# A message-passing layer on one core: one pass over the nodes that writes both node tables

## The chip, the cores and the metric

The kernel runs on one core of a Trainium2 chip. The metric is device time in microseconds (us) of one execution. The kernel before took 5365.72 us, the median of three runs (5353.82, 5365.72 and 5367.68). A profiled execution of the same program, which the profile below describes, took 5379.39 us.

## The reference, cut to what matters

A graph has N = 12500 nodes with 96 features and E = 412500 directed edges, sorted by their destination. Each edge has four attributes.

```python
def _mlp(h, W, b, gamma, beta):
    h = relu(h @ W + b)
    mu, var = mean(h, axis=0), var(h, axis=0)          # over all rows
    return gamma * (h - mu) * rsqrt(var + EPS) + beta

node_feat = _mlp(x, W_node, ...)                        # 12500 x 96
edge_feat = _mlp(edge_attr, W_edge, ...)                # 412500 x 96
message = concatenate([x[row], x[col], edge_feat], 1)   # 412500 x 288
message = _mlp(message, W_msg, ...)
agg = segment_sum(message, col)
out = layernorm(x + agg + node_feat)
```

The product with `W_msg` splits into three blocks of 96 rows, one for the source node, one for the destination node, one for the edge's features. The first two need no edge: `x @ W_msg[0:96]` and `x @ W_msg[96:192]` are computed once for every node and read back by edge. These two products are the node tables, `p_tab` (by source) and `q_tab` (by destination).

## The kernel before, in words

All data is float32. TensorE handles a float32 product in two passes, so a product has two weight loads and two matmul records in the profile. The work has these parts, in the order in which TensorE does them.

1. **The source table** (`table`, lines 140 to 156, called at line 180). The nodes' features lie transposed in SBUF as `xp` (96 x 12544), loaded in seven parts of 14 blocks of 128 nodes. Each block is a stationary operand of 128 columns, and one 96 x 96 block of `w_msg` moves against it. Four blocks share one PSUM tile `pt` (four such tiles, one bank each). VectorE and ScalarE take turns to copy `pt` into the row tile `trow`, which holds 14 blocks (a chunk; three such buffers), and each chunk is written to `p_tab` with one DMA of 672 KB, from SP's queue and from ScalarE's in turn.
2. **A range check** (lines 205 to 219). The destinations `dst` are loaded, made relative to each block's base node (`rel`), reduced to one number on VectorE, transposed with one product on TensorE (`po`, line 216), and turned into a flag.
3. **The destination table** (`table` once more, line 333). It does the same with the second block of `w_msg`, into `q_tab`, with all seven writes from SP's queue. Some 128 rows of zeros are then written around its ends (lines 337 to 340).
4. **Positions** (`places`): four loads, four subtractions on VectorE and four writes to `rel_d`.
5. **The node features** (`nodes`): 25 products `pn` (line 248), a ReLU on ScalarE, statistics on VectorE, the normalised result added to `xp`, then 98 products `py` in groups of eight (line 262), copied as `y0s` and written to `y0_d` (line 269).
6. **The edge statistics** (`edge_norm`, lines 273 to 325): 606 products of 512 columns (`pr`, line 290). Two of them share a tile, on which ScalarE does a ReLU (line 294) and VectorE two `bn_stats` (line 296); such a pair is the unit of this part, 303 in all. Their input `ea` is loaded for eight blocks at a time (line 284), into two buffers.
7. **The messages** (lines 498 to 530): 202 steps, written out by hand for all engines. Each step takes four groups of 512 edges through `edges`, `linear` (z), `message` and `sums`.
8. **The end** (lines 701 to 734): the normalised sum is added to `y0_d`, normalised by row and written.

Beside all this runs GpSimd (POOL). It fetches rows of a table by the edges' source numbers with indirect DMAs, 128 rows each (line 162), called gathers below. The first 26 blocks of 16 gathers go through two `stage` buffers to a scratch area `spill` in DRAM, with one write of 768 KB for each block on SP's queue (line 173). The first three blocks fetch rows of `x` itself; the other 23 fetch from `p_tab` and so wait for all of its seven writes. After the 26 blocks come 100 gathers into a ring of 25 tiles for the first message steps. In the message loop POOL goes on gathering into the ring as its tiles come free.

The orders of SP and POOL are written out by hand in the program (`manual_schedule`); those of TensorE, VectorE and ScalarE before the message loop are made by a scheduler that keeps the program's order nearly everywhere. `next(store)` emits the next block, that is its 16 gathers on POOL and its write on SP, at that place of the two queues. SP works its queue strictly in order: a `spill` write stands behind the loads and writes ahead of it, and those behind it wait until its block has been gathered. A block's gathers need the stage buffer of the block two before, and so that block's write. Each queue issues a DMA only when an earlier one on the same of eight semaphores has landed. In `edge_norm` a block is emitted at 17 of the 26 yields.

Of the kernel before, what the change touches and what calls it, by code (L numbers as in the profile page):

```python
# [11 lines left out]
F32 = mybir.dt.float32  # L12
I32 = mybir.dt.int32
AF = mybir.ActivationFunctionType
# [3 lines left out]
PSUM = bass.MemoryType.PSUM  # L18
DRAM = bass.MemoryType.DRAM

N, C, E, ED = 12500, 96, 412500, 4
EPS = 1e-5
P = 128
# [3 lines left out]
GT, GE, BG = 4, 512, 4  # L27
# [12 lines left out]
NN = NB * P  # L40
NBK = 4
CH = 14
# [5 lines left out]
WN, WS, WM = 31, 16, 7  # L48
# [24 lines left out]
def gnn(ctx, tc, t):  # L73
    nc = tc.nc
    const = ctx.enter_context(tc.tile_pool(name="const", bufs=1))
    dram = ctx.enter_context(tc.tile_pool(name="dram", bufs=1, space=DRAM))
    p_tab = dram.tile([NN, C], F32, name="p_tab")
    q_tab = dram.tile([WT, C], F32, name="q_tab")
# [6 lines left out]
    w_msg = const.tile([C, 3, C], F32, name="w_msg")  # L85
# [4 lines left out]
    xp = xpool.enter_context(tc.tile_pool(name="x", bufs=1)).tile([C, NN], F32, name="xp")  # L90
# [46 lines left out]
        return s[:, 0:1], s[:, 1:2]  # L137


    def table(out, w, work, ps, queues, bufs):  # L140

        rows = out.rearrange("(b p) f -> p b f", p=P)
        for c in range(0, NB, CH):
            r = work.tile([P, CH, C], F32, name="trow", bufs=3)
            for j, i in enumerate(range(0, CH, NBK)):
                n = min(NBK, CH - i)
                pt = ps.tile([P, NBK, C], F32, name="pt", bufs=bufs)
                for g in range(n):
                    k = (c + i + g) * P
                    nc.tensor.matmul(pt[:, g, :], xp[:, k:k + P], w, start=True, stop=True)  # L150
                if j % 2:
                    nc.scalar.activation(r[:, i:i + n, :], pt[:, :n, :], AF.Copy)
                else:
                    nc.vector.tensor_copy(r[:, i:i + n, :], pt[:, :n, :])
            queues[c // CH % len(queues)].dma_start(rows[:, c:c + CH, :], r)
            yield

    def gather(g, pg):
# [17 lines left out]

    store = blocks()
    with tc.manual_schedule(engines={ET.SP, ET.Pool}):
        with tc.tile_pool(name="win_w", bufs=1) as work, tc.tile_pool(name="win_ps", bufs=2, space=PSUM) as ps:
            for i, _ in enumerate(table(p_tab, w_msg[:, 0, :], work, ps, (nc.sync, nc.scalar), 4)):  # L180
                if i in (2, 5):
                    next(store)

    zero = const.tile([64, C], F32, name="zero")
# [5 lines left out]
    for i in range(NS):  # L190
        k, n = Q * i, C - Q * i
# [7 lines left out]
    with tc.tile_pool(name="win", bufs=1) as win, tc.tile_pool(name="win_ps", bufs=2, space=PSUM) as ps:  # L199
# [11 lines left out]
        out = win.tile([P, 1], F32, name="out")  # L211
# [115 lines left out]
    def fast(ring):  # L327
# [1 line left out]
            return gather(g, ring.tile([P, GT, C], F32, name="pg"))  # L329

        with tc.manual_schedule(engines={ET.SP, ET.Pool}):
            with tc.tile_pool(name="tab_w", bufs=1) as work, tc.tile_pool(name="tab_ps", bufs=2, space=PSUM) as ps:
                for i, _ in enumerate(table(q_tab[WM:WM + NN, :], w_msg[:, 1, :], work, ps, (nc.sync,), 8)):
                    if i in (0, 2, 5):
                        next(store)
            next(store)
            nc.sync.dma_start(q_tab[:WM, :], zero[:WM])
            for r in range(WM + NN, WT, 64):
                n = min(64, WT - r)
                nc.sync.dma_start(q_tab[r:r + n, :], zero[:n])  # L340
            places()
            for i, _ in enumerate(nodes()):
                if i in (0, 4, 10):
                    next(store)
            xpool.close()
            n = 0
            for i, _ in enumerate(edge_norm()):
                if 73 * i >= 50 + 100 * n:
                    next(store, None)
                    n += 1  # L350
            for _ in store:
                pass
            got = {g: ahead_of(g) for g in range(SPILL, SPILL + RING)}
# [347 lines left out]
    with tc.tile_pool(name="fin", bufs=2) as work, tc.tile_pool(name="fin_ps", bufs=2, space=PSUM) as ps:  # L701
# [9 lines left out]
        out = t["out"]  # L711
# [57 lines left out]
```

## Time and profile before

| | |
|---|---|
| median of three runs | 5365.72 us |
| the profiled execution's own time | 5379.39 us |
| its span in the profile | 5377.6 us |
| PE busy (matmul records) | 3364.1 us, 63% |
| POOL busy | 3106.6 us, 58% |
| VectorE (DVE) busy | 1699.3 us, 32% |
| ScalarE (ACT) busy | 1077.6 us, 20% |
| DMA, mean | 50 GB/s |
| gathers from a table | 3175, some 0.95 us each |

The busy shares are means over stages that differ. The table of stretches that the prediction shows is read in this way: the stretch in us, its length, then busy time and number of instructions of PE, the weight loads, DVE, ACT and POOL, then the granted TensorE clock, the share of the DMA engines and GB/s. In a list by time, each line has the start, the length, engine, line and tile; the bracket at its end is the time that the engine stood idle before it, and what ended that. "issue" means that nothing in the profile explains the idle time, "remote" that the releasing event could not be assigned.

### The profile page before, as it was taken

Reading aid. Unit: us, or ns where it says so; the run is one execution under the profiler, and the core shown is the slowest. Engines: PE = TensorE matmul, PEld = TensorE weight load, DVE = VectorE, ACT = ScalarE, POOL = GpSimd, SP = SyncE. Lnnn points to the kernel's source line nnn. Section 1 sums busy time; section 2 is a strip of 40 time slices with the busy share of each in tenths; the row PEclk is TensorE's granted clock in tenths of the full one; section 3 lists DMA queues with packets and bytes.
Section 4 is the critical chain, followed back from the end, with each engine's and each line's share of the span. In section 5 each row is a group of like instructions: output and inputs, shape, how many; then the busy total and the mean of one; then the engine's idle time right before and its main releaser. Section 6 shows DMA issues by size and latency. Waiting matters only on the chain. (4 is left out here: it accounts for less than half of the span.)

```text
span 5377.6 us, 46715 instructions
## 1 busy us (share of the span) xinstructions
PE 3364.1 (63%) x16705; PEld 2570.3 (48%) x16705; DVE 1699.3 (32%) x2622; ACT 1077.6 (20%) x1015; POOL 3106.6 (58%) x3244
## 2 busy tenths in 40 slices
PE   5566662666656666665667666656666666666668
PEld 5333330354545545544445554544455545545447
DVE  1445551622222322222222322322232222223225
ACT  0224441411111111111111111111111111111112
POOL 5454456155566656666666666666666666666661
PEclk9755555566666766667676766666766666666667
DMA  5332332111111111111111111111111111111112
GB/s 165 112 97 61 71 68 48 29 33 37 39 44 38 43 42 44 43 38 42 42 43 45 42 38 43 44 42 45 37 43 42 41 45 36 43 43 42 44 37 84
DMA packets 188578, 270.80 MB, mean 50 GB/s; under 512 B 121095, under 2 KB 121480, under 8 KB 187330
## 3 DMA queue, kind: packets, MB, share of 16 engines
q0 software_dynamic: 103136, 158.62, 12.2%
q1 hardware_dynamic: 77120, 98.40, 6.6%
q10 hardware_dynamic: 8080, 10.71, 0.7%
q8 instruction: 133, 2.18, 0.2%
q14 instruction: 109, 0.89, 0.1%
HBM read 225.90 MB, written 41.60 MB: 50 GB/s over the span
## 5 line engine op out<-in xcount | busy, mean ns | idle before, releaser
L162 POOL DMA_INDIRECT pg<-p_tab,src x2807 | 2690.8, 959 | 1767.1 <-DVE hs L463 922.8
L448 PE MATMUL z<-rhs,left 128*128 128x96 f32 x6446 | 1222.7, 339 | 878.3 <-issue 672.8
L448 PEld LDWEIGHTS z<-rhs,left 128*128 128x128 f32 x6446 | 1093.2, 249 | 1183.6 <-issue 903.1
L480 PE MATMUL pa<-h 128*97 128x128 f32 x6446 | 1246.3, 331 | 556.2 <-issue 551.6
L480 PEld LDWEIGHTS pa<-h 128*97 128x97 f32 x6446 | 1015.4, 209 | 654.7 <-issue 653.3
L463 DVE TENSOR_TENSOR hs<-z,pg 128x384 f32<-128x384 f32 x702 | 385.2, 555 | 2599.2 <-remote 1537.6
L465 ACT ACTIVATE h<-hs 128x768 f32<-128x768 f32 x402 | 338.9, 843 | 2867.6 <-DVE hs L463 1846.0
L290 PE MATMUL pr<-ea,wide 10*128 10x512 f32 x1212 | 405.4, 1074 | 285.7 <-issue 177.6
L162 POOL DMA_INDIRECT stage<-p_tab,src x368 | 351.0, 954 | 369.6 <-DMA spill<-stage 240.0
L440 ACT ACTIVATE left<-pr 96x2048 f32<-96x2048 f32 x202 | 377.2, 1867 | 643.6 <-remote 439.7
L441 DVE TENSOR_SCALAR left<-pr 31x2048 f32<-31x2048 f32 x202 | 462.9, 2291 | 108.3 <-ACT left L440 75.5
L296 DVE BATCH_NORM_STATS2 estats<-r 128x6 f32<-128x512 f32 x606 | 365.8, 678 | 326.8 <-issue 191.1
L433 PE MATMUL pr<-ea,we 6*127 6x512 f32 x1404 | 411.1, 808 | 62.6 <-issue 47.5
L290 PEld LDWEIGHTS pr<-ea,wide 10*128 10x128 f32 x1212 | 209.6, 320 | 480.2 <-issue 291.8
L294 ACT ACTIVATE r<-pr 128x1024 f32<-128x1024 f32 x303 | 297.1, 1024 | 458.0 <-remote 290.0
L433 PEld LDWEIGHTS pr<-ea,we 6*127 6x127 f32 x1404 | 117.9, 223 | 206.6 <-issue 190.6
L457 DVE TENSOR_TENSOR h<-rel,iota 128x496 f32<-128x496 f32 x202 | 134.6, 666 | 0.0
L463 DVE TENSOR_TENSOR hs<-z,pb 128x384 f32<-128x384 f32 x104 | 56.6, 554 | 233.1 <-remote 85.2
L150 PE MATMUL pt<-w_msg,xp 96*128 96x96 f32 x392 | 88.7, 421 | 60.4 <-issue 37.1
L493 DVE TENSOR_TENSOR agg<-pa,agg 97x62 f32 x404 | 90.1, 223 | 85.4 <-remote 54.8
L150 PEld LDWEIGHTS pt<-w_msg,xp 96*128 96x128 f32 x392 | 85.5, 330 | 63.4 <-issue 48.6
L494 DVE TENSOR_TENSOR gram<-pa,gram 97x388 f32<-97x388 f32 x202 | 111.4, 551 | 0.1
(107 smaller groups left out, 634.7 us busy)
## 6 DMA issues: line engine op xcount, KB each, us to landing
pg<-p_tab,src POOLq DMA_INDIRECT x2807
spill<-stage SPq DMA_DIRECT2D x26, 768.0 KB
pb<-spill SPq DMA_DIRECT2D x26, 768.0 KB
ea<-in_ea SPq DMA_DIRECT2D x75, 160.0 KB
rhs<-q_tab SPq DMA_DIRECT2D x202, 46.5 KB
ea<-in_ea SPq DMA_DIRECT2D x352, 20.0 KB
stage<-p_tab,src POOLq DMA_INDIRECT x368
q_tab<-trow SPq DMA_DIRECT2D x7, 672.0 KB
```

What stands on the lines that cost most here:

```text
L150: nc.tensor.matmul(pt[:, g, :], xp[:, k:k + P], w, start=True, stop=True)
L162: nc.gpsimd.indirect_dma_start(out=pg[:, i, :], out_offset=None, in_=tab[:, :], in_offset=bass.IndirectOffsetOnAxis(ap=idx[:, k:k + 1], ax ...
L290: nc.tensor.matmul(pr[:, k % 2, :], wide[Q * i:Q * i + 2 * EK, :], ea[Q * i:Q * i + 2 * EK, b % J, :], start=True, stop=True)
L294: nc.scalar.activation(r, pr, AF.Relu)
L296: nc.vector.bn_stats(stats[:, (k - o) % NS, (k - o) // NS, :], r[:, 1 - o, :])
L433: nc.tensor.matmul(prs[s][:C + WN, i, :], we[Q * i:Q * i + EK + 1, :], block[s][Q * i:Q * i + EK + 1, :], start=True, stop=True)
L440: nc.scalar.activation(x[:C, :n, :], pr[:C, :n, :], AF.Relu)
L441: nc.vector.tensor_scalar(x[C:C + WN, :n, :], pr[C:C + WN, :n, :], 0.0, None, op0=OP.is_equal)
L448: nc.tensor.matmul(zs[k][:, i, :], left[s % 2][:KR, g % BG, i * P:(i + 1) * P], rhs[:KR, s % RB, g % BG, :], start=True, stop=True)
L463: nc.vector.tensor_add(hs[:, i % 2, :n, :], z[:, :n, :], pg[:, :n, :])
L465: nc.scalar.activation(h[:, i - 1:i + 1, :, :C], hs, AF.Relu)
L480: nc.tensor.matmul(pas[s][:, g % BG, :C + 1 + WN], h[:r, i, :C + 1], h[:r, i, :C + 1 + WN], start=i == 0, stop=i == n - 1)
```

## The change

Both tables are made in one pass. The two 96-column blocks of `w_msg` lie side by side and move together, 192 columns, against each stationary block of nodes. A PSUM tile is now two banks (still four blocks of nodes, four such tiles, so all eight banks), and each copy carries both tables' rows for its blocks. The row tile holds both tables and has two buffers instead of three. Each chunk is written with two DMAs of 672 KB, one for each table, one from SP's queue and one from ScalarE's, in turn. The places of the blocks' gathers and writes in the orders of SP and POOL move as well: before the edge statistics eight blocks are emitted instead of nine, so 18 instead of 17 come in them. The zero rows of `q_tab` and with them the load of `dst` follow the last table write.

```diff
-    def table(out, w, work, ps, queues, bufs):
-        rows = out.rearrange("(b p) f -> p b f", p=P)
+    def tables(work, ps):
+        outs = [t.rearrange("(b p) f -> p b f", p=P) for t in (p_tab, q_tab[WM:WM + NN, :])]
+        w = w_msg[:, 0:2, :].rearrange("k s f -> k (s f)")
         for c in range(0, NB, CH):
-            r = work.tile([P, CH, C], F32, name="trow", bufs=3)
+            r = work.tile([P, CH, 2, C], F32, name="trow", bufs=2)
             for j, i in enumerate(range(0, CH, NBK)):
                 n = min(NBK, CH - i)
-                pt = ps.tile([P, NBK, C], F32, name="pt", bufs=bufs)
+                pt = ps.tile([P, 2, GE], F32, name="pt")
                 for g in range(n):
                     k = (c + i + g) * P
-                    nc.tensor.matmul(pt[:, g, :], xp[:, k:k + P], w, start=True, stop=True)
+                    nc.tensor.matmul(pt[:, g // 2, g % 2 * 2 * C:(g % 2 + 1) * 2 * C], xp[:, k:k + P], w,
+                                     start=True, stop=True)
+                to = r[:, i:i + n, :, :].rearrange("p (k b) s f -> p k (b s f)", b=2)
                 if j % 2:
-                    nc.scalar.activation(r[:, i:i + n, :], pt[:, :n, :], AF.Copy)
+                    nc.scalar.activation(to, pt[:, :n // 2, :4 * C], AF.Copy)
                 else:
-                    nc.vector.tensor_copy(r[:, i:i + n, :], pt[:, :n, :])
-            queues[c // CH % len(queues)].dma_start(rows[:, c:c + CH, :], r)
+                    nc.vector.tensor_copy(to, pt[:, :n // 2, :4 * C])
+            for k in range(2):
+                (nc.scalar if (c // CH + k) % 2 else nc.sync).dma_start(outs[k][:, c:c + CH, :], r[:, :, k, :])
             yield
...
-        with tc.tile_pool(name="win_w", bufs=1) as work, tc.tile_pool(name="win_ps", bufs=2, space=PSUM) as ps:
-            for i, _ in enumerate(table(p_tab, w_msg[:, 0, :], work, ps, (nc.sync, nc.scalar), 4)):
-                if i in (2, 5):
+        with tc.tile_pool(name="win_w", bufs=1) as work, tc.tile_pool(name="win_ps", bufs=4, space=PSUM) as ps:
+            for i, _ in enumerate(tables(work, ps)):
+                if i in (2, 4):
                     next(store)
...
         with tc.manual_schedule(engines={ET.SP, ET.Pool}):
-            with tc.tile_pool(name="tab_w", bufs=1) as work, tc.tile_pool(name="tab_ps", bufs=2, space=PSUM) as ps:
-                for i, _ in enumerate(table(q_tab[WM:WM + NN, :], w_msg[:, 1, :], work, ps, (nc.sync,), 8)):
-                    if i in (0, 2, 5):
-                        next(store)
-            next(store)
             nc.sync.dma_start(q_tab[:WM, :], zero[:WM])
             for r in range(WM + NN, WT, 64):
                 n = min(64, WT - r)
                 nc.sync.dma_start(q_tab[r:r + n, :], zero[:n])
+            next(store)
             places()
+            next(store)
+            next(store)
             for i, _ in enumerate(nodes()):
-                if i in (0, 4, 10):
+                if i in (1, 5, 10):
                     next(store)
```

## The prediction

> **What bounds the kernel now.** I read the chain of waits first; it covers only the last 1%. So I cut the span into the program's parts and read busy times by stretch (columns: PE, PEld, DVE, ACT, POOL, then clock, DMA share, GB/s).
>
> ```profile
> 0.00:87.00 87.00, 43.68 (x196) 42.26 (x196) 8.33 (x20) 6.82 (x15) 46.67 (x56) 1.00 0.66 177
> 87.00:174.00 87.00, 45.35 (x197) 43.30 (x197) 19.46 (x28) 5.22 (x14) 47.71 (x48) 1.00 0.41 123
> 174.00:226.00 52.00, 30.71 (x50) 9.54 (x50) 20.59 (x33) 18.51 (x28) 30.85 (x32) 0.73 0.42 131
> 226.00:305.00 79.00, 43.71 (x196) 42.26 (x196) 36.32 (x26) 13.37 (x10) 30.27 (x32) 0.50 0.30 106
> 305.00:915.00 610.00, 338.89 (x994) 171.51 (x996) 297.07 (x496) 239.66 (x245) 336.77 (x356) 0.50 0.31 68
> 915.00:995.00 80.00, 66.51 (x220) 38.05 (x216) 64.23 (x109) 55.62 (x57) 0.00 (x0) 0.50 0.16 31
> 995.00:1047.00 52.00, 7.37 (x36) 5.24 (x36) 32.66 (x34) 4.02 (x4) 0.83 (x1) 0.50 0.03 9
> 1047.00:5300.00 4253.00, 2728.80 (x14486) 2160.80 (x14486) 1182.12 (x1802) 715.27 (x611) 2595.40 (x2707) 0.68 0.16 41
> ```
>
> The change touches the first 995 us only. The message loop (1047 to 5300) keeps its instructions in their order on every engine. The stretches are: source table, destination table, node features (two), edge statistics while POOL still gathers, the same after POOL's end (915), its closing sums, and the loop. The page's share "PE 63%" is thus a mean mostly over the loop; here PE was busy for half of the two table stretches.
>
> Next, PE by time, with the destination table.
>
> ```profile
> 107.47 29.75 PE L150 MATMUL pt<-w_msg,xp 96*128 96x96 f32 x138 [0.37 <-DVE most L218]
> ...
> 152.92 0.32 PE L150 MATMUL pt<-w_msg,xp 96*128 96x96 f32 x1 [2.48 <-issue]
> ...
> 165.54 8.41 PE L150 MATMUL pt<-w_msg,xp 96*128 96x96 f32 x38 [0.18 <-issue]
> 174.37 18.80 PE L248 MATMUL pn<-xp,w_node 96*96 96x512 f32 x36 [0.42 <-ACT trow L152]
> ```
>
> From 107.47 there are 138 passes in 29.75 us, 0.216 us each. Then one pass comes only every 2.8 us for "issue", and from 165.54 it is dense again. POOL's gathers at that time:
>
> ```profile
> 87.57 0.94 POOL L162 DMA_INDIRECT stage<-p_tab,src  x1 [18.26 <-DMA we<-step]
> ...
> 120.57 0.95 POOL L162 DMA_INDIRECT stage<-p_tab,src  x1 [11.00 <-DMA spill<-stage]
> ...
> 159.35 0.95 POOL L162 DMA_INDIRECT stage<-p_tab,src  x1 [0.30 <-issue]
> 175.58 0.95 POOL L162 DMA_INDIRECT stage<-p_tab,src  x1 [15.29 <-DMA spill<-stage]
> ```
>
> A gather starts every 1.25 us from 120.57 to 160.3. PE thins out 17 us after this train began and recovers 5 us after its end. The same holds in the source table, on DVE (train to 69.3):
>
> ```profile
> 38.80 1.02 DVE L154 COPY trow<-pt 128x384 f32<-128x384 f32 x2 [10.85 <-DMA p_tab<-trow]
> ...
> 56.81 0.56 DVE L154 COPY trow<-pt 128x384 f32<-128x384 f32 x1 [14.84 <-remote]
> 74.45 1.02 DVE L154 COPY trow<-pt 128x384 f32<-128x384 f32 x2 [17.08 <-remote]
> ```
>
> The copies at 56.81 and 74.45 waited 15 and 17 us; after the train ended all went on. Edge statistics, two stretches of 10 us:
>
> ```profile
> 480.00:490.00 10.00, 2.07 (x4) 0.51 (x4) 1.29 (x2) 1.02 (x1) 7.56 (x9) 0.50 0.16 39
> 600.00:610.00 10.00, 10.00 (x38) 5.85 (x37) 10.00 (x18) 8.63 (x10) 0.00 (x0) 0.50 0.10 14
> ```
>
> With POOL gathering, ten us hold 4 PE records, that is one pair; with POOL idle, 38. In the thin mode a pair takes 11.2 us, in the dense one 1.19 us (212 records, 53 pairs, in the 62.94 us from 931.96). I call this the thin mode: it sets in 12 to 17 us after a long train begins and ends 5 us after it. Its cause is not in the profile. It means that work beside POOL's trains is nearly stopped, and that the early part lasts about as long as the trains (468 gathers after `p_tab`, 585 us) plus the dense work outside them.
>
> **The change part by part.** I count against the profiled 5379.4 us (span 5377.6, 1.8 outside), which is 13.7 above the median of 5365.7; the saving is then taken off the median.
>
> *Products.* 392 passes of 96 columns become 196 of 192. A `pn` pass (512 moving columns, 96 stationary) took 18.80/36 = 0.522 us. Against 0.216 this is 0.307 us for 416 columns more, so 96 more cost 0.07 to 0.08, bounded by 0 and by 0.216 (nothing saved). I take 0.29 a pass, 0.58 a product, 8.1 us for a chunk of 14, where one table's chunk took 6.0. In sum 57 us instead of 85.
>
> *Copies.* 56 become 28 of double width. On DVE the `y0s` copy has just this shape and took 0.947 us, against 0.557: 14 x 0.947 = 13.3 instead of 15.6. On ACT 768 columns lie between 0.491 (384) and 1.024 (1024 columns); I take 0.80: 9.0 instead of 11.5. They lie beside the next products (8.1 us a chunk against 1.9 and 1.3). Without that cover they add some 2 us a chunk.
>
> *Writes and buffers.* The 14 writes stay, seven now on each queue. With two row buffers a chunk's first copy waits for both writes of the chunk two before. Before, with three, the first such wait was 10.85 us long (38.80), for a write issued at 33.74: 5 us to landing. That write stood behind small constant loads on SP; one more load now stands ahead of it (0.4 us). So chunk 2 is copied at about 40, although its products are done by 9.0 + 3 x 8.1 = 33. From there each chunk needs 8.1 us of PE; two chunks (16.2) cover copies, issue and landing (3 + 0.4 + 5), so writes add nothing unless landing takes 13 us. Four more chunks of products and their last copies end near 40 + 5 x 8.1 = 81, landed 86, against the first gather from `p_tab` at 87.57.
>
> The skill's page "Perfetto Trace Analysis", section Optimization Strategy, speaks against this part: repeated bubbles on the engine that should be full can mean too few buffers for the next tile. By it five chunks would each show a wait; at 15 us to landing it would be 1.1 us a chunk, 5 us in all, where the row of 5 us gives none.
>
> The page "TensorE: Matmul & The Clock Gate", Part 1, has the array at half clock until some 3.4 us of sustained work. Passes here stayed at 0.216 us for 29.75 us on end, while eight `z` passes of the same width took 0.87 us at 1116.22. By the page, warm passes would take some 4 us off each of five chunks, 20 us in all, an estimate; the sum keeps the measured rate.
>
> *The thin mode in this stage.* Before, 27 us passed between 47.3 and 74.45 with 16 of 196 passes done. The third raw block now has to wait for the first block's spill write, which moved behind chunk 2's write (issued at 37.76 before, now at 43 or later), so POOL's train breaks for some us near 50. Between no stretch (86) and the old one kept whole (113) I take half: `p_tab` complete at 99, +11.4 us.
>
> *The second table's stage goes.* From the first gather (87.57) to `pn` (174.37) were 86.8 us, of which 20 (load of `dst`, reductions, `po` until 107.47) stay, as PE still runs `po` ahead of `pn`. So 66.8 us go. The zero rows' three writes (1 us each) stand ahead of `dst` now, but it waits for the table writes to land anyway. `pn` starts at 99 + 20 = 119 instead of 174.4: -55.4.
>
> *Node features* took 131 us (174.37 to 305) beside 64 gathers. They now meet a train from 99 to 139 (blocks 3 and 4), whose spill writes stand behind the positions' writes on SP, and a second from some 146 to 186. Passes still owed at 2.8 us would add up to 25 us; against that, PE at 107.47, also 20 us into a train, ran dense. The first two `y0_d` writes wait for block 4's spill (near 141), while before they were ready 17 us after the statistics, here past 180: hidden. I take +10 (0 to 25). Edge statistics start at 260 instead of 305: -45.
>
> *Edge statistics* get one block more, 16 gathers, 20 us. A lone train costs the thin part, 20 - 13 + 5 = 12 us. The upper bound is a whole period: from 387.09 to 550.80 POOL's starts are five blocks apart, 33 us each. The lower bound is 0, as the trailing 80 us without POOL (915 to 995) could take it. I take +12. POOL's end moves by -45 and one period, 33, to 903, the statistics' to 995 - 45 + 12 = 962; so POOL isn't late for the loop, where it waited 131 us.
>
> Sum: +11.4 - 66.8 + 10 + 12 = -33 us. 5365.7 - 33 = 5333.
>
> **The rivals.**
>
> *More is won* (5298 to 5318): no thin stretch in the table stage (-13) and none new in the node features (-10). For it: the broken train. Against: POOL starts the same 48 raw gathers at the same time.
>
> *Nothing is won* (5350 to 5380): the 67 us held 40 us of gathers, which must go elsewhere and slow what stands there. Old thin stretch kept (+14), node features +25 instead of +10, gives -4: 5362. Here belongs also that a wide pass costs two narrow ones (0.43): four or five chunks x 4 us, -15.
>
> *Slower*: the node products fall into the thin mode. 50 passes at 2.8 us are 140 us instead of 50; with +90 in place of +10 the sum is +47: 5413. It decides from some 26 passes more than the 14 that were thin before (33 + 10 + 16 = 59 us, at 2.28 us extra a pass). For it: they now start 20 us into a 40 us train. Against: after block 6 (near 186) POOL must wait for a spill that stands behind the first two `y0_d` writes, so the mode is broken twice.
>
> **How the numbers follow.** Three runs of the kernel differ by 0.26%, so about 0.3% (16 us) can be told from no change. Chances: forecast (5318 to 5349) 0.48, more won 0.21, nothing won 0.19, slower 0.12. All low costs together give 5365.7 - 33 - 13 - 10 - 12 = 5298; run scatter puts the end at 5293. The upper end, 5375, takes in nothing won but for its highest edge cost (+21 on -4 would be 5383); with the slower case and what lies below 5293 some 0.2 are left out. Faster 0.69, same 0.19, slower 0.12.
>
> **What would show it.** Right: 196 table passes of about 0.29 us; the first gather from `p_tab` between 86 and 113; `pn` 20 us after it; the first `pr` product near 260; the last one near 962; loop of the same length, 33 us earlier. Wrong: `pn` records 2.8 us apart for more than 50 us; DVE copies waiting over 13 us for table writes at each chunk; POOL's last ring gather after the edge statistics; a loop that differs by over 15 us.

## The result and the profile after

The changed kernel took 5296.60 us, the median of four runs (5291.13 to 5302.76); the kernel before took 5361.52 us beside it. The ratio is 0.9884, with a 95% interval of 0.9868 to 0.9900, so 65 us were won. The forecast was 33 us. The profiled execution has a span of 5294.2 us.

The stretches of the changed kernel, in the columns of the table shown for the kernel before (stretch, length, PE, weight loads, DVE, ACT, POOL, clock, DMA share, GB/s), cut at the same events:

```profile
0.00:81.00 81.00, 41.76 (x196) 39.80 (x196) 13.92 (x20) 10.17 (x15) 46.56 (x57) 0.81 0.94 251
81.00:102.00 21.00, 0.40 (x2) 0.10 (x2) 11.55 (x14) 0.00 (x0) 16.43 (x16) 0.50 0.51 154
102.00:142.00 40.00, 28.34 (x50) 9.11 (x50) 17.21 (x26) 14.33 (x21) 30.55 (x32) 0.71 0.54 171
142.00:244.00 102.00, 43.71 (x196) 42.26 (x196) 41.28 (x40) 17.43 (x16) 55.49 (x60) 0.50 0.35 105
244.00:883.00 639.00, 369.49 (x1092) 184.84 (x1092) 324.99 (x538) 261.75 (x269) 342.21 (x363) 0.50 0.32 68
883.00:935.00 52.00, 37.06 (x120) 19.79 (x120) 35.71 (x60) 31.71 (x33) 0.00 (x0) 0.50 0.08 13
935.00:983.00 48.00, 4.00 (x18) 2.03 (x18) 31.10 (x32) 3.33 (x4) 0.00 (x0) 0.50 0.03 6
983.00:5240.00 4257.00, 2823.15 (x14640) 2204.56 (x14639) 1196.81 (x1836) 719.48 (x618) 2583.14 (x2707) 0.68 0.18 41
```

The first line now holds all passes for both tables: 196, as many as the source table alone had, and PE is busy for 41.76 us where it was for 43.68. The next one, 21 us, is all that is left between the first gather from `p_tab` and the node products; it was 86.8 us. TensorE by time, changed kernel:

```profile
9.55 10.28 PE L151 MATMUL pt<-w_msg,xp 96*128 96x192 f32 x44 [9.55 <-DMA xp<-in_xp]
...
39.94 16.95 PE L151 MATMUL pt<-w_msg,xp 96*128 96x192 f32 x84 [5.58 <-DVE trow L157]
58.60 6.50 PE L151 MATMUL pt<-w_msg,xp 96*128 96x192 f32 x28 [1.71 <-DVE trow L157]
...
101.98 20.17 PE L252 MATMUL pn<-xp,w_node 96*96 96x512 f32 x40 [0.37 <-DVE most L222]
```

The first 44 wide passes came in 10.28 us, 0.234 each, and the last four chunks (112 passes) in 25.2 us, with one wait of 1.71 us between. There is no thin stretch on TensorE. POOL's list by time, same execution:

```profile
53.37 0.94 POOL L166 DMA_INDIRECT stage<-in_x,src_raw  x1 [5.88 <-DMA spill<-stage]
...
80.96 0.94 POOL L166 DMA_INDIRECT stage<-p_tab,src  x1 [7.93 <-issue]
```

The third raw block had to wait 5.88 us (from 47.5) for the first block's spill write, which SP had issued at 41.99. So the raw train broke, and the first gather from `p_tab` started at 80.96 in place of 87.57. Of the thin mode one long wait was left, in ScalarE's last copy, with the last table write behind it (ScalarE by time):

```profile
73.81 0.49 ACT L155 ACTIVATE trow<-pt 128x384 f32<-128x384 f32 x1 [8.66 <-remote]
74.33 0.46 ACTq L159 DMA_DIRECT2D q_tab<-trow  x1
```

Where the time went, by stage. The last columns are from the experiments below: one profile of the kernel before (e9) and two of the changed kernel (e5, e10) on a second chip, where the kernel before takes 5392 to 5396 us. Each entry is a difference of two start times read from the lists by time.

| stage | forecast | recorded runs: before, after | change | second chip: before | after (e5, e10) | change |
|---|---|---|---|---|---|---|
| start to first gather from `p_tab` | +11.4 | 87.6, 81.0 | -6.6 | 89.2 | 85.3, 82.1 | -4.0, -7.1 |
| to first `pn` | -66.8 | 86.8, 21.0 | -65.8 | 87.7 | 21.2, 21.1 | -66.5, -66.6 |
| to first `pr` (node features) | +10 | 135.4, 142.3 | +6.9 | 125.4 | 174.9, 172.8 | +49.6, +47.4 |
| to the end of the last wide `pr` | +12 | 685.1, 690.5 | +5.4 | 695.9 | 682.2, 682.5 | -13.7, -13.4 |
| to first `z` | 0 | 48.4, 47.9 | -0.5 | 48.4 | 47.8, 47.8 | -0.6 |
| sum at first `z` | -33 | 1043.3, 982.7 | -60.6 | 1046.5 | 1011.3, 1006.3 | -35.2, -40.2 |
| loop, to `norm_msg` | 0 | 4279.6, 4256.9 | -22.7 | 4294.0 | 4286.7, 4300.9 | -7.3, +6.9 |

In the recorded runs 60.6 us are there when the message loop starts, against 65 us between the medians. The profiled execution of before was a long one (5379.4 against a median of 5361.5); if these 18 us lie in its loop, they are most of the loop's -22.7. Two profiles of one program differ by 14 us in that row (e5, e10).

### The profile page after: what moved, and what is told of

Same layout as the page of the kernel before. It is cut to its first block, busy times and chain, and to the rows that moved or that the text cites. A ratio compares the mean times of both kernels' runs of the same rounds, so it can differ in the third digit from the quotient of the medians.

```text
span 5294.2 us, 46278 instructions
## 1 busy us (share of the span) xinstructions
PE 3390.6 (64%) x16509; PEld 2544.8 (48%) x16509; DVE 1697.4 (32%) x2608; ACT 1071.9 (20%) x1001; POOL 3092.4 (58%) x3244
## 5 line engine op out<-in xcount | busy, mean ns | idle before, releaser
L482 PE MATMUL pa<-h 128*97 128x128 f32 x6446 | 1230.0, 331 | 473.0 <-issue 470.2
L435 PE MATMUL pr<-ea,we 6*127 6x512 f32 x1404 | 508.9, 883 | 92.6 <-issue 79.8
L435 PEld LDWEIGHTS pr<-ea,we 6*127 6x127 f32 x1404 | 144.5, 242 | 291.0 <-issue 278.8
L735 POOL TENSOR_TENSOR y<-y,sd 128x768 f32<-128x768 f32 (+1 forms) x13 | 18.0, 1394 | 107.7 <-DVE sd L734 105.7
L435 PE MATMUL pr<-eae,we 6*127 6x512 f32 x208 | 64.7, 820 | 10.8 <-issue 9.7
```

The costliest lines, as they stand in the source:

```text
L435: nc.tensor.matmul(prs[s][:C + WN, i, :], we[Q * i:Q * i + EK + 1, :], block[s][Q * i:Q * i + EK + 1, :], start=True, stop=True)
L482: nc.tensor.matmul(pas[s][:, g % BG, :C + 1 + WN], h[:r, i, :C + 1], h[:r, i, :C + 1 + WN], start=i == 0, stop=i == n - 1)
```

## The experiments

Two theories of the source table's stage are set against each other. TRAINS: what is done beside a train of gathers older than some 15 us is slowed to the thin mode, so it matters where POOL's trains are cut. FEWER PASSES (first named FEWER INSTRUCTIONS): the gain is TensorE's work that is no longer done. For the later stages the rival of TRAINS is LOAD: the number of gathers costs what it costs, wherever and however long they run.

The chips differed more than the kernels. The kernel before took 5392 to 5396 us on the second chip (e5 to e12) and 4164 to 4165 us on two others (e1 to e4; e13 to e18), where the thin mode was not found. The first expectations had not reckoned with that. The chip of the recorded runs has no number on record; that it is not the second one is read from the times alone, 5353.8 to 5367.7 us there against 5374.2 to 5410.8 on the second.

### e1, two products; e2, early spill; e3, late spill in the kernel before; e4, three row buffers (no thin mode)

```diff
# e1: for each node block, on the changed kernel
-nc.tensor.matmul(pt[:, g // 2, g % 2 * 2 * C:(g % 2 + 1) * 2 * C], xp[:, k:k + P], w, ...)
+for s in range(2):
+    o = (g % 2 * 2 + s) * C
+    nc.tensor.matmul(pt[:, g // 2, o:o + C], xp[:, k:k + P], w_msg[:, s, :], ...)
# e2: on the changed kernel           # e3: on the kernel before
-    if i in (2, 4):                  -    if i in (2, 5):
+    if i in (1, 3):                  +    if i in (4, 5):
# e4: on the changed kernel
-RING = 25                            -r = work.tile([P, CH, 2, C], F32, name="trow", bufs=2)
+RING = 21                            +r = work.tile([P, CH, 2, C], F32, name="trow", bufs=3)
```

> One pass over the nodes as in the changed kernel, the same copies and writes, but two products of 96 columns for each node block in place of one of 192. TRAINS (the table pass became quick because POOL's gathers were cut into trains of 18 to 20 us): the pass count matters only by its dense cost. 392 passes at 0.216 us are 85 us against 196 at 0.234 (46 us, 44 passes in 10.28 us in the changed kernel), so a chunk costs 12.1 us instead of 6.6. The first gather from the source table moves from 81.0 to about 105, as five chunks lie behind the first wait; the total is 20 to 28 us above the changed kernel, about 5320. FEWER INSTRUCTIONS (it became quick because half as many passes were left to be thinned out): passes 2.8 us apart appear in the table pass, the first gather comes at 115 or later, the total is 35 us or more above, 5332 or more.

> The changed kernel with the first two blocks emitted one and one chunk earlier, so that the first spill write stands ahead of the third chunk's write and POOL's raw gathers run on without a pause from 29 to about 70, as in the kernel before. TRAINS: thin mode returns from about 45 to 75, copies on VectorE and ScalarE wait 12 us or more there, the first gather from the source table moves from 81 to 91 to 100, and the total is 8 to 18 us above the changed kernel: 5305 to 5315. FEWER INSTRUCTIONS: no such waits, first gather at 78 to 84, total 5293 to 5300.

> The kernel before, both tables in two passes, with only the first block emitted two chunks later, so that its spill write stands behind the fifth chunk's write and POOL pauses after 32 raw gathers (about 48 to 58). TRAINS: the waits of 15 and 17 us on VectorE vanish, the first gather from the source table comes at 72 to 80 instead of 87.6, the total falls by 7 to 15 us against the kernel before. FEWER INSTRUCTIONS: thin mode stays, first gather at 85 or later, the total within 5 us of the kernel before.

> The changed kernel with three row buffers instead of two; to make room the ring has 21 tiles instead of 25, so the message loop is not to be compared, only the table pass. BUFFERS BIND: TensorE's idle time in the table pass (5.4, 5.6 and 1.7 us before the passes at 32.7, 39.9 and 58.6) goes, the table pass ends 8 to 12 us sooner (last pass at 53 to 57 instead of 65.1). BUFFERS DO NOT BIND, as the prediction said: the writes' queue sets the pace, the last pass comes at 61 to 66.

The kernel before took 4163.84 us. e1: 4182.10 (ratio 1.0047, 1.0031 to 1.0064). e2: 4157.38 (0.9985, 0.9976 to 0.9995). e3: 4164.98 (1.0003, 0.9993 to 1.0013). e4: 4160.82 in a single run. With no thin mode there is nothing for TRAINS to act on, so these runs leave it open. They show that the change is worth little there (6.5 us in e2) and that two narrow products lose it and more. With a third row buffer the last wide pass ended at 61.0, against 62.5 in e2 and 64.9 in e16 (the changed kernel as it is, on the other chip without the thin mode), and the first gather from `p_tab` came at 75.27, against 73.46 and 74.25. So the third buffer moves the passes by 1.5 to 4 us and nothing behind them; e4's whole time has a smaller ring in it and is not to be compared. In e1 the first gather from `p_tab` stood at 100.26 against 73.46 in e2, 26.8 us later; the end came 24.7 us later.

### e5 and e10, the changed kernel; e9, the kernel before (second chip)

No edit.

> The changed kernel once more, with nothing altered, to see what the change is worth on the chip that these runs are on. Two answers are prepared, told apart by the time of the kernel before in the same call. If the kernel before takes near 5360 us there (TensorE, VectorE and ScalarE issue one pass in some 2.8 us beside long trains of gathers, the thin mode): ratio 0.985 to 0.991, 48 to 80 us won, first gather from p_tab at 78 to 84 us, first pn pass at 98 to 106, first pr pass at 235 to 255. If the kernel before takes near 4164 us (no thin mode): the second table's stage was 43 us of dense passes there (80 to 123 us) on TensorE, while GpSimd's gathers set the end, so 2 to 12 us won, ratio 0.997 to 0.9995, first gather from p_tab at 72 to 80 us, first pn pass near 95, first pr pass near 197. The theory that the gain is TensorE work removed (196 passes by 0.21 us, 42 us) wants 35 to 45 us won on either chip.

> The kernel before, unaltered, for one profile on the chip of these runs, so that the change can be read stage by stage on a second chip. If its time is above 5300 us: first gather from p_tab at 80 to 92 us, first pn pass at 170 to 195, first pr pass at 300 to 335, first z pass at 1035 to 1065. Theory STAGES (the gain is the second table's stage and the first gather, and the node and edge stages cost about the same in both kernels): the difference to the changed kernel at the first pn pass is 60 to 85 us and at the first z pass 40 to 75. Theory PHASE (how far the thin mode reaches into the node and edge stages depends on where POOL's trains happen to fall, so the same program shifts by tens of us): the first pr pass or the first z pass is over 15 us from 309.8 or 1043.3 while the first pn pass is within 10 us of 174.4. If its time is near 4164 us: first gather from p_tab near 74 to 80, first pr near 238, first z near 648.

> The changed kernel, unaltered, for one more profile beside that of the kernel before. With thin mode: first gather from p_tab at 78 to 88 us, first pn pass 20 to 22 later, first pr pass at 240 to 285, first z pass at 980 to 1015 (two earlier profiles had 80.96, 244.31, 982.66 and 85.26, 281.35, 1011.31); theory PHASE says that first pr and first z move by over 15 us from one profile to the next, theory STAGES that they stay within 10. Without thin mode: first pr near 197, first z near 629.

e5: 5354.67 against 5392.31 us, ratio 0.9935 (0.9912 to 0.9958), 37.6 us won. e9: 5396.98; e10: 5363.61 (a single run each). The 37.6 us miss the 48 to 80 that were prepared for a kernel before near 5360 us. They are in the 35 to 45 that TensorE's removed work wanted, but not for that reason: the second table's stage is gone for 66.6 us here too, and the node features give 48 back. PHASE, that each profile shifts by tens of us, falls: e9 is within 8 us of the recorded profile at `pn`, `pr` and `z`, and e10 within 5.4 us of e5. STAGES holds up to `pn` (70.5 us won with e5, 73.7 with e10, of 60 to 85) and fails behind it, as the node features cost some 48 us more in the changed kernel. It is these that differ between the recorded runs and this chip. TensorE in e10:

```profile
103.19 14.33 PE L252 MATMUL pn<-xp,w_node 96*96 96x512 f32 x26 [0.37 <-issue]
120.36 2.02 PE L252 MATMUL pn<-xp,w_node 96*96 96x512 f32 x2 [2.84 <-issue]
...
172.17 2.73 PE L252 MATMUL pn<-xp,w_node 96*96 96x512 f32 x4 [1.48 <-ACT agg L253]
...
276.01 20.99 PE L294 MATMUL pr<-ea,wide 10*128 10x512 f32 x60 [34.10 <-DMA ea<-in_ea]
```

The first 26 of 50 `pn` passes are dense (40 in the recorded profile); then a pair comes every 5.6 us, 20 passes in all, until 172. The list of DVE adds the second loss, in the copy of the last full group of `py`:

```profile
239.73 0.96 DVE L270 COPY y0s<-py 128x768 f32<-128x768 f32 x1 [7.30 <-PE py L266]
266.46 0.96 DVE L270 COPY y0s<-py 128x768 f32<-128x768 f32 x1 [25.78 <-remote]
```

That copy stood still for 25.78 us, the write behind it on SP too, and the first load of `ea` behind both; `pr` waited 34.10 us for that load. In the recorded profile the copy waited 8.93 us. Early in this train one gather takes 3.1 us instead of 0.95 in both profiles. From the next one (95.59 here, 94.36 recorded) to the end of the dense passes it was 22 us here and 28 in the recorded profile; counted from the train's first gather it was 35 and 41 us. So the 12 to 17 us that the prediction read off are no fixed age of a train. Why the mode sets in when it does is not in the profiles.

### e6, two products, on the second chip

The edit of e1.

> The changed kernel with two 96-column products for each node block in place of one of 192 columns: 392 passes into the same tiles, same copies, same writes. Theory FEWER PASSES: each pass costs 0.21 to 0.24 us whatever its width, so the 196 more cost 41 to 46 us of TensorE in the table stage, which were the sources' gathers' wait: first gather from p_tab 15 to 30 us later than in the changed kernel, and 15 to 30 us more at the end, on a chip with thin mode as on one without (there 4182 against 4157 us for the nearest one-product kernel). Theory TRAINS (only with the kernel before near 5360 us): the passes that fall beside a train of gathers older than 15 us come once in 2.8 us, so the table stage stretches by 40 us or more, and the time is within 0.3% of the kernel before or slower.

5385.17 us, ratio 0.9989 (0.9972 to 1.0006): 30.5 us more than the changed kernel (e5). TensorE by time:

```profile
9.45 38.05 PE L153 MATMUL pt<-w_msg,xp 96*128 96x96 f32 x177 [9.45 <-DMA xp<-in_xp]
```

And POOL by time, from the third raw block:

```profile
63.24 0.95 POOL L168 DMA_INDIRECT stage<-in_x,src_raw  x1 [14.29 <-DMA spill<-stage]
...
109.36 0.95 POOL L168 DMA_INDIRECT stage<-p_tab,src  x1 [26.42 <-DMA q_tab<-zero]
```

177 narrow passes took 38.05 us, 0.215 each, as long as the wide ones (41.76/196 = 0.213 in the recorded profile). The first gather comes 24.1 us later than in e5. FEWER PASSES holds for this part. TRAINS' stretch by 40 us did not come, as the train broke here too, for 14 us; that the time is within 0.3% of the kernel before fits TRAINS as well and decides nothing.

### e7, early spill, on the second chip

The edit of e2, which leaves POOL's raw train in one piece.

> The changed kernel with the second raw block of gathers queued one chunk earlier (after the fourth chunk of the tables in place of the fifth), so that its wait for the staging buffer stands ahead of one chunk's q_tab write on the queue, and POOL's train of raw gathers is cut less. Theory TRAINS (with the kernel before near 5360 us): the train is 15 us old while two chunks' passes are still to come, these come at 2.8 us, first gather from p_tab at 95 us or later, 14 to 60 us slower than the changed kernel. Theory FEWER PASSES: the passes stay at 0.21 to 0.24 us, first gather from p_tab at 70 to 82, within 10 us of the changed kernel. On a chip with the kernel before near 4164 us both say the same: 0 to 5 us faster than the changed kernel.

5369.78 us, ratio 0.9958 (0.9941 to 0.9975): 15.1 us more than e5, with the same passes. TensorE by time:

```profile
39.49 9.09 PE L151 MATMUL pt<-w_msg,xp 96*128 96x192 f32 x36 [5.41 <-issue]
67.78 6.07 PE L151 MATMUL pt<-w_msg,xp 96*128 96x192 f32 x20 [19.20 <-issue]
```

VectorE's third copy in that time:

```profile
66.76 0.96 DVE L157 COPY trow<-pt 128x768 f32<-128x768 f32 x1 [22.58 <-remote]
```

And POOL, the last raw gather and the first from `p_tab`:

```profile
66.69 0.94 POOL L166 DMA_INDIRECT stage<-in_x,src_raw  x1 [0.30 <-issue]
96.39 0.94 POOL L166 DMA_INDIRECT stage<-p_tab,src  x1 [28.76 <-DMA q_tab<-zero]
```

The raw train ran from 3.1 to 67.6 with no pause over 1.5 us. The thin mode came with it: no pass from 48.6 to 67.8, and a copy that waited 22.58 us. The first gather from `p_tab` is at 96.39 in place of 85.26. TRAINS holds, at the lower end of its price.

### e11, late spill in the kernel before, on the second chip

The edit of e3, which cuts the raw train without wide products.

> The kernel before with its first raw block's spill and the third block's gathers queued two chunks later (after the fifth and sixth chunk of the source table in place of the third and sixth), so that POOL's train of raw gathers breaks for 4 to 6 us near 48 without the wide products. With thin mode, theory TRAINS: the stretch of 27 us with 16 of 196 passes goes, first gather from p_tab at 70 to 80 in place of 87, and 6 to 18 us are won by this alone (ratio 0.9967 to 0.999), which is the part of the change's gain that wide products have no part in. Theory FEWER PASSES: the gather stays at 85 to 92 and the time within 5 us of the kernel before. Without thin mode: within 5 us.

5380.63 us, ratio 0.9966 (0.9948 to 0.9984), 15.3 us won by the cut alone (8.6 to 28 by the interval). POOL by time:

```profile
57.74 0.95 POOL L162 DMA_INDIRECT stage<-in_x,src_raw  x1 [10.69 <-DMA spill<-stage]
...
80.15 0.95 POOL L162 DMA_INDIRECT stage<-p_tab,src  x1 [0.30 <-issue]
```

The train broke for 10.69 us, and the first gather from `p_tab` came at 80.15 against 89.21 in e9; the first `z` at 1030.3 against 1046.5. So on this chip the cut by itself is worth 15 of the 38 us that the change is worth, and e7 shows the same 15 from the other side.

### e8, a memset behind each gather (second chip)

```diff
 nc.gpsimd.indirect_dma_start(out=pg[:, i, :], ...)
+nc.gpsimd.memset(pause, 0.0)          # pause: 128 x 64
```

> The changed kernel with a memset of 128 x 64 on GpSimd after each of its 3200 gathers. On a chip without thin mode, where gathers follow each other by 1.25 us with 0.30 of it not busy, the memset (0.10 to 0.15 us by the rows of small memsets, 0.20 for 128 x 128) adds 0 to 0.2 us to each: 0 to 600 us more. On a chip with thin mode: if it is the nearly gapless train that starves the other engines' issue, a train with a gap of the memset in each step does so less, passes beside it come faster than one in 2.8 us, and the edge statistics (650 us before the last pr pass in the changed kernel) shorten by more than 100 us though GpSimd does more; if the load of gathers alone does it, they stay within 50 us of that or lengthen.

5352.83 us in a single run, against 5354.67 (e5). The memsets took 0.168 us each, 543 us of POOL in sum, and the whole time did not move. Its parts did: the first `z` came 28 to 34 us earlier (977.8 against 1011.3 and 1006.3 in e5 and e10), and the loop took 18 to 32 us more (4318.6 against 4286.7 and 4300.9) for the 472 us of memsets in it. So POOL bounds this chip's loop in small part at most. The edge statistics took 669 us in place of 682. A gap of 0.17 us between gathers does not stop the thin mode, then; the break of 5.02 us in e5 did, as e7 shows.

### e12, fewer blocks gathered ahead (second chip)

```diff
-SPILL = 26 * BG
+SPILL = 14 * BG
```

> The changed kernel with 14 in place of 26 blocks of gathers put ahead of the message loop; the other 12 are gathered in the loop. With thin mode: in the edge statistics each block costs the other engines 13 to 20 us, so first z comes 130 to 240 us earlier; the loop (4257 us with 2807 gathers, POOL idle for 1729 us of it) takes 192 more. If the loop is not held by POOL (adding 0.17 us of POOL work to each gather left the time where it was), it lengthens by less than 100 us and the whole is 60 to 240 us faster than the changed kernel. If its length follows the number of gathers (1.52 us each), it lengthens by 290 us and the whole is 50 to 160 us slower. Without thin mode, where POOL's gathers set the loop (1.24 us each): 100 to 240 us slower.

5411.55 us, ratio 1.0028 (1.0014 to 1.0042), 48 to 57 us more than the changed kernel's two profiles' runs. Stretches, with the columns as above:

```profile
276.00:535.00 259.00, 106.38 (x284) 44.07 (x284) 82.20 (x134) 66.42 (x68) 155.09 (x164) 0.50 0.26 58
535.00:810.00 275.00, 274.42 (x928) 186.05 (x928) 274.77 (x464) 237.37 (x235) 0.00 (x0) 0.50 0.23 36
...
858.00:5351.00 4493.00, 2788.84 (x14640) 2236.95 (x14640) 1198.05 (x1835) 720.29 (x617) 2781.98 (x2899) 0.67 0.16 39
```

The edge statistics fell from 682 to 533 us, 12.4 us for each of the 12 blocks: with POOL silent (second line) PE was busy for 274.42 of 275 us, beside gathers (first line) for 106 of 259. The loop grew by 192 to 206 us, about 1.04 us for each of its 192 more gathers. Both answers that were prepared for the loop missed: it follows its gathers in part. The first `z` came 148 to 153 us earlier, as forecast.

### e13 and e17, one staging buffer; e14, half blocks; e15 and e18, fewer gathers beside the node products; e16, the changed kernel (no thin mode)

```diff
# e13, e17
-pg = ring.tile([P, BG, GT, C], F32, name="stage", bufs=2)
+pg = ring.tile([P, BG, GT, C], F32, name="stage", bufs=1)
# e14: two tiles [P, 2, GT, C] with bufs=1 a block, each with its own spill write
# e15, e18
 places()
-next(store)
-next(store)
 for i, _ in enumerate(nodes()):
-    if i in (1, 5, 10):
+    if i in (1, 4, 7, 10):
...
-        if 73 * i >= 50 + 100 * n:
+        if 77 * i >= 50 + 100 * n:
```

> The changed kernel with one staging buffer in place of two for the blocks that are gathered ahead: the next block's gathers wait until the last block's spill has landed, so no train is longer than one block, 20 us, and pauses of 4 to 8 us stand between. Same gathers, same products. With the kernel before near 5395 us, theory TRAINS (the thin mode needs a train of 17 to 22 us and ends 5 us after it): at most 8 us of thin mode a block in place of 12.4, and none where PE work is short; edge statistics 500 to 600 us in place of 682, node features (first pn to first pr) 110 to 150 in place of 173, first gather from p_tab up to 15 us later; 90 to 230 us faster than the changed kernel. Theory LOAD (the number of gathers alone sets what is lost): edge statistics 650 us or more, and the pauses come on top, 0 to 60 us slower than the changed kernel. With the kernel before near 4164 us: 0 to 130 us slower.

> The changed kernel with the blocks gathered ahead cut in two halves in one staging buffer of half the size, each half with its own spill write: trains of 8 gathers, 10 us, with 4 to 6 us between. With the kernel before near 5395 us, theory TRAINS: no thin mode at all before the message loop; node features 95 to 115 us in place of 173; edge statistics held by POOL's 18 blocks of 30 us, 480 to 580 in place of 682; 150 to 260 us faster than the changed kernel. Theory LOAD: edge statistics 650 us or more, time within 60 us of the changed kernel or slower.

> The changed kernel with the two spill writes ahead of the node features moved behind the second and fifth group of node products (and one block more left to the edge statistics): POOL's train from p_tab ends after two blocks, some 40 us after its first gather, in place of four blocks. With the kernel before near 5395 us, theory TRAINS: pn passes stay dense but for a few near the train's end, first py pass 15 to 30 us earlier, first pn to first pr 120 to 150 us in place of 173, edge statistics 5 to 20 us longer, 10 to 45 us faster than the changed kernel. Theory LOAD: first pn to first pr within 12 us of 173, time within 12 us of the changed kernel or slower.

> The changed kernel unaltered, beside the three others. With the kernel before near 5395 us: 25 to 50 us faster than it (ratio 0.991 to 0.9955), node features 165 to 180 us; near 5360 us: 48 to 80 us faster, node features 135 to 150; near 4164 us: 2 to 12 us faster.

> The changed kernel with one staging buffer in place of two, once more. With the kernel before near 5395 us (or 5360): TRAINS says edge statistics 500 to 600 us in place of 682, node features 110 to 150 in place of 173, 60 to 230 us faster than the changed kernel (5355 to 5364 there); LOAD says edge statistics 650 us or more and 0 to 100 us slower than it. With the kernel before near 4164 us: 4331, as before, since each pause of the gathers then counts.

> The changed kernel with the two spill writes ahead of the node features moved into them, once more. With the kernel before near 5395 us (or 5360): TRAINS says first pn to first pr 115 to 150 us in place of 173, edge statistics 5 to 25 us longer, 10 to 50 us faster than the changed kernel; LOAD says first pn to first pr within 12 us of 173 and the time within 12 us of the changed kernel or slower. With the kernel before near 4164 us: 4199, as before.

All six fell on a chip without the thin mode, so what they were meant for, the node features' term, stays open. There the kernel before took 4164.68 us (4164.20 with e17, e18). e16: 4157.99, ratio 0.9983 (0.9973 to 0.9992), 6.7 us won. e13: 4331.21 (1.0405, 1.0388 to 1.0423) and e17: 4333.04 (1.0404). e14: 4424.25 (1.0628, 1.0610 to 1.0646). e15: 4198.76 (1.0085, 1.0069 to 1.0102) and e18: 4199.79 (1.0078). For this kind of chip e13 was expected 0 to 130 us above the changed kernel and came 173 above; e16, e17 and e18 came as expected. They show what bounds the kernel there. The list of waits (who waits for whom: us in total, times, longest), for e13:

```profile
POOL stage L166 <- DMA spill<-stage: 175.4, 24, 25.0
```

The same line of e15:

```profile
POOL stage L166 <- DMA spill<-stage: 39.7, 3, 34.1
```

e13 is 173 us slower than e16 with 175.4 us of such waits, e15 41 us slower with 39.7 (e16 has 5.0), e14 266 us with 303.9. POOL's gathers follow one another to the end, and a pause is paid in full or nearly so. Hence, it seems, the change wins little: it starts them hardly earlier. (The kernel before has no profile there; e3 stands in for it.) Its first gather from `p_tab` is at 74.25 in e16; in e3, as fast as the kernel before (ratio 1.0003), it was at 73.32. The second table's stage is gone in e16 (first `z` at 628.7 against 648.4 in e3), but both loops end within 1.1 us of each other. A stretch of ten us in e16 stands against the line 480 to 490 of the kernel before, where PE had 4 records:

```profile
480.00:490.00 10.00, 10.00 (x39) 5.43 (x36) 10.00 (x18) 8.26 (x9) 7.44 (x9) 0.50 0.25 52
```

Nine gathers, as there, at the same granted clock of 0.50, and PE has 39 records.

## Why the prediction was right and wrong

*Second table's stage, -66.8.* Right: -65.8 in the recorded runs, -66.5 and -66.6 on the second chip. What stays is the 21 us from the first gather to `pn`, forecast as 20.

*Source table, +11.4.* Wrong, and the step that failed: -6.6, 18 us off, over half of the error. Two terms of the step were mis-sized. (1) The products, the larger one: the step had the last copies end at 40 + 5 x 8.1 = 81. The wide pass was taken as 0.29 us, on a straight line between passes of 96 and of 512 columns; it measured 0.234 over the first 44 and 41.76/196 = 0.213 over all. And the sum counts five chunk times where four chunks were left: at 39.94 TensorE had done 84 of 196 passes, and the other four chunks took 25.2 us, where the sum allows 40.5 for them and their last copies. Without the thin mode's wait the last copies would have ended near 66, an estimate from 65.10, where the last pass ended. That is 15 of the 18 us. (2) The thin mode: the step took half of the old stretch of 27 us, +13, because POOL's train would break "for some us". It broke for 5.88 us, and the stretch was gone but for one copy's 8.66 us, so 4 to 5 us less than forecast. On the second chip e7 and e11 show what the break is worth from both sides: the uncut train puts the first gather at 96.4 and costs 15 us, the cut alone wins 15. The last copies came at 68 us on VectorE and 74 on ScalarE, and the sign named for this step, a first gather between 86 and 113, failed. The row that would have told (1) is the weight loads' in the kernel before, here for its dense stretch of narrow passes (columns as above):

```profile
107.00:137.00 30.00, 29.63 (x139) 29.54 (x139) 4.33 (x9) 2.96 (x7) 14.43 (x17) 1.00 0.48 146
```

Loads fill 29.54 of 30 us, as do the passes (29.63). The reading that fits is that at 96 columns the next load, 0.21 us, sets the pace, and 96 more moving columns hide in it. At 512 columns (`pn`: 9.54 us of loads beside 30.71 of passes, in the table shown before) the loads are short of the passes. e6's narrow passes, at the same 0.215 us as the wide ones, fit this too; that the load is the cause was not tried by itself. Why a load takes 0.21 us here is open: the eight `z` passes that the prediction names took 0.11 us each, with a load for each pass and the granted clock at 1.00 in both stretches.

The Trainium skill, page "Perfetto Trace Analysis", section Identifying the Most-Contended Engine, says that TensorE's headroom is to be judged by the rate of its useful arithmetic and by the busy share of its weight loads, and not by the busy share of its matmuls. In this row both shares are full, 29.54 and 29.63 of 30 us, so it does not set one measure above the other. Taken as the limit, the full loads would have put the wide pass at 0.216 us. The bubbles of the page's Optimization Strategy, which the prediction priced at 5 us, are there: VectorE's first copy waited for table writes at each of the last five chunks (15.83, 2.82, 1.92, 4.90 and 5.08 us), where the prediction expected it at the first of them alone. The writes issued at 49.70 and 52.90 held copies until 57.59 and 64.49, 8 and 12 us in place of 5. TensorE itself, once it went on at 39.94, lost 1.71 us to this. Three row buffers (e4) brought the first gather no earlier, on a chip without the thin mode. The 20 us for a warm clock, from "TensorE: Matmul & The Clock Gate", were not to be had: in the stretch just shown, and in the prediction's own table for both table stretches, the granted clock was 1.00 already, and the passes still took 0.216 us.

*Node features, +10 (0 to 25).* Inside the bounds in the recorded runs (+6.9) and far outside on the second chip (+47 to +50). The upper bound, 25 us, counted passes still owed at 2.8 us; there 20 of 50 fell into the thin mode, and one copy of `y0s` held up the load of `ea`. This is the mechanism of the rival *slower*, at half its price, and the largest term between the 38 and the 65 us won (40 to 43 us, of which the edge statistics give 19 back). Why the mode sets in 6 us sooner there than in the recorded profile is open, and so is whether an earlier end of the train (e15) would help there.

*Edge statistics, +12 (0 to 12).* +5.4, and -13.5 on the second chip, below the lower bound: a block more in a stage does not cost a block's time in it. Twelve fewer saved 12.4 us each (e12), the price that the step used, so the price of a block is right as a mean but not for the one at the edge.

*The sum.* The recorded case lies just below the rival *more is won* (5298 to 5318): all low costs at once gave 5298, and it took 5296.6. That it comes so near is in part luck. The reason given for that rival, the broken train, is true, but it is worth 4 to 5 us beyond the half that the forecast had credited; the products' 15 us, which the rival does not name, did more, and the node features and the edge block cost 7 and 5 us where all low costs at once had none. The kernel before was also 4.2 us faster beside the changed one than when the forecast was made. On the second chip the sum -33 came out nearly right, -37.6, by luck: from terms that missed by 15 to 18, 37 to 40 and 25 to 26 us in different directions. The loop was forecast to keep its length. On the second chip it did, within the 14 us by which two profiles of one program differ; the recorded pair's -22.7 is beyond the 15 us named as a sign, and the long profile before may be most of it.

## What to carry to other kernels

Before pricing a wider product, hold the weight loads' time against the passes' in the same stretch: where they were equal here, going from 96 to 192 moving columns was free (0.216 and 0.213 us a pass). Where work beside a train of gathers nearly stops, ask of each change first where the trains are cut after it, since writes moved on a queue were worth 15 us here with no product removed (e11), half of what the 196 passes were worth (30.5 us, e6). A gain read off one chip can be bound to it: the same change was worth 65, 38 and 7 us, the last where POOL's gathers set the end.

## What the runs showed of the hardware

The same program took 5361 us in the recorded runs, 5392 to 5396 on a second chip and 4164 to 4165 on two others. What goes with the difference is the thin mode: without it, ten us with nine gathers hold 39 PE records instead of 4, and the message loop takes 3476 us (e16) instead of 4257 to 4301. In that loop, too, the kernel before has passes 1.4 us apart beside a train (2000.38 to 2007.36); that the mode makes up all of the loop's difference is not shown. The granted clock does not explain the ten us: it is 0.50 in both of those stretches. What sets the mode, and why some chips lack it, the profiles do not show; whether the engines' instructions reach them late beside a train (the page of the kernel before counts 242 packets on its two instruction queues) was not tried. Where the mode exists, 543 us of memsets on POOL left the whole time as it was, and gathers cost the edge statistics 12.4 us for each block of 20 us (e12). Where it does not, POOL's gathers are the bound, and pauses of 175 and 304 us in them cost 173 and 266.
